# An edge loop of a graph layer: score pieces and codes moved earlier in the hand-written order, and one-hots turned by a product of code columns

## Chip, cores and metric

The kernel runs on one core of a Trainium2 chip. The metric is the device time of one execution in microseconds (us), the median of several runs. Engines are named as the profile names them: PE (TensorE, with PEld its weight loads), DVE (VectorE), ACT (ScalarE), POOL (GpSimd, which here issues the gathers), SP (SyncE, which issues other DMAs).

## The reference, cut to what matters

The whole program is a stack of four graph layers, each followed by a feed-forward layer with experts, over 1250 nodes of 512 features and 20000 edges sorted by target node. The change is in the second graph layer (L1), attention over the edges with four heads:

```
h = (x @ W).reshape(n, 4, 128)
alpha = leaky_relu(a_src[src] + a_dst[dst] + a_edge, 0.2)    # one score per edge and head
amax  = segment_max(alpha, dst)
ex    = exp(alpha - amax[dst])
denom = segment_sum(ex, dst)
out   = segment_sum(h[src] * (ex / (denom[dst] + 1e-16)), dst) + bias
```

After it come a normalisation over the nodes and the residual sum. Everything is float32 from outside.

## The kernel before, in words

The edges are laid out in groups of 512, each padded so that all its targets lie in one block of 125 nodes. 46 groups are run without a condition, as 23 pairs (group A is the even one of a pair, B the odd one); four more groups stand under a condition (L1836) that this input does not meet. A table t1 in device memory holds for each node the 4 x 129 features (with a column of ones) and four source scores.

For a group g the loop `l1_edges` (L1688 to L1918) does these steps, each a small function:

- `gathers` (L1709, the DMA is L428): POOL issues four indirect DMAs that bring the 512 source rows into G. The buffer ring has eight groups.
- `onehot` (L1720): DVE compares target numbers with 0..124 and makes `oh`, 128 edges x 4 x 125 nodes, float32.
- `pieces` (L1725): for a pair, DVE adds the gathered source score and the edge score, and splits the float32 sum into three bfloat16 pieces (two adds L1732, then L1735, L1737, L1738, L1739). They go into columns 15 to 26 of CD; columns 0 to 14 hold the seven bits of the target's number, their complements and a one, made once in `edge_bits`.
- `coded` (L1741): PE transposes CD, eight blocks a pair, into `pc`, and ACT copies it to R: 27 rows x 1024 edges, bfloat16 (L1746).
- `spread` (L1754): for each head, one product of SEL (27 x 125) with R. It yields, for each node and edge, the edge's score if the edge has that target and a huge negative number if not.
- `maxima` (L1759): DVE takes the maximum along the edges, four reductions (L1765), then five small steps that update the running maximum of the block; `mn` is a copy for the next step.
- `turned` (L1748): PE transposes `oh`, four transposes into the PSUM bank `tr` (L1750), and ACT copies them to `ohT` (L1752).
- `fetched` (L1781): products with `ohT` as weights bring each edge its target's score and maximum (L1784). Float32 products appear as two PE instructions each. The results lie in the bank of the fourth head's spread.
- `lowered`, `weights_of` (L1775, L1787): the factors by which old sums shrink, and the weights ex of the edges (DVE L1790 to L1793, ACT L1794).
- `scaled`, `scaled_v` (L1800, L1806): ACT (28 instructions of 128x129 a pair) and DVE (one block a pair) multiply G by ex.
- `summed` (L1810): products of `oh` with G, 16 PE instructions a group, into the two banks `ac` (L1814).
- `added` (L1818): DVE adds them to the running sums ACC (L1823).

Three pairs are in flight: in turn i the loop computes the weights of pair i, sums pair i-1, takes the maxima of pair i+1, makes the pieces and codes of pair i+2, and starts the gathers of pair i+3. The order in which DVE, ACT and PE do these steps is written out by hand (L1857 to L1918): each engine gets its instructions in the order of the calls and runs them in that order, waiting where an operand is missing. In a turn with i >= 0 the order is, for PE: spread A (pair i+1), sums A (i-1), spread B, turned A, sums B, turned B, codes (i+2), fetched A and B. For DVE: weights (i), maxima A (i+1), one scaled block, adds A (i-1), maxima B, pieces (i+2), adds B, one-hots (i+2). For ACT: the exponential, five scaled blocks, the copy for turned A, two scaled blocks, the copy for turned B, the copy of R, the two lowering steps. POOL's gathers are not in the hand-written order but need free buffers, so they follow the sums.

`edge_bits` (L1638) runs much earlier, among the first expert layer's work: it makes the bit columns of CD, and SEL by four small transposes (L1683).

Of the kernel before, what the change touches and what calls it, by code (L numbers as in the profile page):

```python
# [9 lines left out]
F32 = mybir.dt.float32  # L10
F16 = mybir.dt.float16
BF16 = mybir.dt.bfloat16
# [3 lines left out]
AF = mybir.ActivationFunctionType  # L16
OP = mybir.AluOpType
# [6 lines left out]
P = 125  # L24
NT = N // P
EJ = E // P
GS = 512
# [9 lines left out]
class Net:  # L37
# [1600 lines left out]
    def edge_bits(self):  # L1638

        nc, ES, f = self.nc, self.ES, self.g1  # L1640
        nh, nb = 4, 7
        C = 2.0 ** 100
        nr = f.nr = 2 * nb + 1


        CD = f.CD = f.p.tile([128, ST, nr + 3 * nh], BF16, name="g1cd")
        SEL = f.SEL = f.p.tile([nr + 3 * nh, nh, P], BF16, name="g1sel")
        with ExitStack() as c3:
            r = self.pool(c3, "g1b")
            T = r.tile([128, nh, nr + 3 * nh], F32, name="g1t")  # L1650
            xp = r.tile([128, 1], I32, name="g1xp0")
            d0 = r.tile([128, ST], F32, name="g1d0")

            for t in (T[0:1, 0, 0:1], xp[0:1, :], d0[0:1, 0:1]):
                nc.vector.tensor_copy(t, self.S1[0:1, 0, 0:1])
            nc.vector.tensor_scalar(d0, ES[:, :, 1], float(2 ** nb - 1), None, OP.min)
            x = r.tile([128, ST], I32, name="g1x0")
            nc.vector.tensor_copy(x, d0)
            nc.vector.tensor_copy(xp, self.iota_p)
            nc.vector.memset(T, 0.0)  # L1660
            nc.vector.memset(T[:, :, 2 * nb:nr], -float(nb) * C)
            for h in range(nh):
                for j in range(3):
                    o = nr + j * nh + h
                    nc.vector.memset(T[:, h, o:o + 1], 1.0)
            nc.vector.memset(CD[:, :, 2 * nb:nr], 1.0)
            bt = r.tile([128, nb], F32, name="g1bt")
            xs = [x, r.tile([128, ST], I32, name="g1x1")]
            for b in range(nb):
                y = xs[1 - b % 2]  # L1670
                nc.vector.tensor_scalar(y, x, 1, None, OP.logical_shift_right)
                nc.vector.scalar_tensor_tensor(CD[:, :, b], y, -2.0, x, OP.mult, OP.add)
                nc.vector.tensor_scalar(CD[:, :, nb + b], CD[:, :, b], -1.0, 1.0, OP.mult, OP.add)
                yp = r.tile([128, 1], I32, name=f"g1yp{b}")
                nc.vector.tensor_scalar(yp, xp, 1, None, OP.logical_shift_right)
                nc.vector.scalar_tensor_tensor(bt[:, b:b + 1], yp, -2.0, xp, OP.mult, OP.add)
                x, xp = y, yp
            nc.vector.tensor_scalar(T[:, :, 0:nb], bt[:, None, :].to_broadcast([128, nh, nb]), C, None, OP.mult)
            nc.vector.tensor_scalar(T[:, :, nb:2 * nb], bt[:, None, :].to_broadcast([128, nh, nb]), -C, C,
                                    OP.mult, OP.add)  # L1680
            for h in range(nh):
                ps = self.bank("g1sel_ps")
                nc.tensor.transpose(ps[:nr + 3 * nh, :P], T[:P, h, :], self.ident[:P, :P])  # L1683
                nc.vector.tensor_copy(SEL[:, h, :], ps[:nr + 3 * nh, :P])
            identb = f.identb = f.p.tile([128, 128], BF16, name="g1id")
            nc.vector.tensor_copy(identb, self.ident)

    def l1_edges(self, ctx):  # L1688
# [4 lines left out]
        nc, tc, ES, SI, f = self.nc, self.tc, self.ES, self.SI, self.g1  # L1693
        nh, ch, nr = 4, 128, f.nr
        tw = nh * (ch + 1) + nh
        ACC, AM, AE, t1, CD, SEL, identb = f.ACC, f.AM, f.AE, f.t1, f.CD, f.SEL, f.identb
        gq = self.pool(ctx, "g1g", bufs=8)
        q8 = self.pool(ctx, "g1h", bufs=8)
        q4 = self.pool(ctx, "g1p", bufs=4)
# [4 lines left out]
        tr = self.bank("oht_ps")  # L1704

        mg = mx[3][:, :16 * nh].rearrange("p (k h) -> p k h", k=8)
        st, pr = {}, {}

        def gathers(g, after=False):  # L1709
            G = gq.tile([128, 4, tw], F32, name="G")  # L1710
            ix, o = SI, 4 * g
            if after:

                ix, o = q8.tile([128, 4], I32, name="ix"), 0
                nc.vector.tensor_copy(ix, SI[:, 4 * g:4 * g + 4])
            for k in range(4):
                self.gather(G[:, k, :], t1, ix[:, o + k:o + k + 1])
            st[g] = {"G": G}

        def onehot(g):  # L1720
            oh = st[g]["oh"] = q8.tile([128, 4, P], F32, name="oh")
            nc.vector.tensor_tensor(oh, self.iota[:, None, :P].to_broadcast([128, 4, P]),
                                    ES[:, 4 * g:4 * g + 4, 1:2].to_broadcast([128, 4, P]), OP.is_equal)
# [22 lines left out]
            nc.scalar.copy(pr[i]["R"][:, j0 * GS:j1 * GS], pc[:nr + 3 * nh, j0 * GS:j1 * GS])  # L1746

        def turned(g):  # L1748
            for k in range(4):
                nc.tensor.transpose(tr[:P, k * 128:(k + 1) * 128], st[g]["oh"][:, k, :], self.ident)  # L1750
            ohT = st[g]["ohT"] = q4.tile([P, GS], F32, name="ohT")
            nc.scalar.copy(ohT, tr[:P, :])  # L1752

        def spread(g):  # L1754
            for h in range(nh):
# [72 lines left out]
        def at(f, i, *args):  # L1828
            if 0 <= i < NP:
                f(i, *args)  # L1830

        def one(f, i, j, *args):
            if 0 <= i < NP:
                f(2 * i + j, *args)
# [22 lines left out]
        with self.tc.manual_schedule(engines={E.DVE, E.Activation, E.PE}):  # L1857
            for j in range(2):
                gathers(j)
                onehot(j)  # L1860
                turned(j)
            for i in range(-2, NP + 1):


                at(weights_of, i)
                if i >= 0:
                    one(spread, i + 1, 0)
                kv = 2 if i == NP - 1 else 1
                one(scaled, i, 0, range(kv, 4))
                if i >= 0:  # L1870
                    one(maxima, i + 1, 0)
                if i in (-1, 0):
                    one(gathers, i + 3, 0, True)
                for k in range(kv):
                    one(scaled_v, i, 0, k)
                one(summed, i - 1, 0)
                if i > 0:
                    one(gathers, i + 3, 0)
                one(spread, i + 1, 1)
                one(added, i - 1, 0)  # L1880
                if i == NP - 1:
                    for k in range(2):
                        one(scaled_v, i, 1, k)
                else:
                    one(scaled, i, 1, range(0, 2))
                if i >= 0:
                    one(turned, i + 1, 0)
                one(scaled, i, 1, range(2, 4))
                one(summed, i - 1, 1)
                if i > 0:  # L1890
                    one(gathers, i + 3, 1)
                one(maxima, i + 1, 1)
                if i in (-1, 0):
                    one(gathers, i + 3, 1, True)
                if i == -1:
                    for j in range(2):
                        one(onehot, i + 2, j)
                if i == -2:
                    for j in range(2):
                        at(pieces, i + 2, j, j + 1)  # L1900
                        at(coded, i + 2, j, j + 1)
                        one(gathers, i + 3, j, True)
                        if j == 0:
                            one(spread, i + 2, 0)
                            one(maxima, i + 2, 0)
                else:
                    at(pieces, i + 2, 0, 2)
                if i >= 0:
                    one(turned, i + 1, 1)
                if i > -2:  # L1910
                    at(coded, i + 2)
                for j in range(2):
                    one(fetched, i + 1, j)
                at(lowered, i + 1)
                one(added, i - 1, 1)
                if i >= 0:
                    for j in range(2):
                        one(onehot, i + 2, j)  # L1918
# [468 lines left out]
```

## Time and profile before

| | us |
|---|---|
| median of 3 runs | 2721.48 |
| lowest and highest | 2719.5, 2733.79 |
| the profiled execution | 2716.28 |
| its span, first to last instruction | 2714.5 |
| PE busy in the span | 2444.6 (90%) |
| DVE busy | 1419.5 (52%) |
| mean granted TensorE clock | 0.923 |
| edge loop, 3rd to 22nd pair's start | 882.12 to 1172.61 |

How to read what follows: the timeline's lines give the start, the length, the engine, the line of the kernel, the operation, what it writes and reads, the shapes, and how many instructions were merged; in brackets stands the idle time before and what ended it. A line of the stretches gives from and to, the length, the busy time of each engine with the count of its instructions, the granted clock of PE as a share of full speed, the share of DMA engines in use and GB/s. A line of the waits gives who waited for whom, the total, how often, and the longest.

### The profile page before, as it was taken

The page shows a single profiled execution, that of the slowest core. Times are in us where ns is not written, and L with a number is a line of the kernel's source. Part 1 is how long each engine was busy: PE and PEld are TensorE (multiplying, and loading weights), DVE is VectorE, ACT ScalarE, POOL GpSimd, SP SyncE. Part 2 cuts the span into 40 slices and gives each one's busy share as a digit, 9 for nine tenths or more (in the row PEclk, how much of TensorE's full clock was granted, in tenths as well). Part 3 has the DMA queues.
Part 4 walks back from the last instruction along what each step waited for, and adds up shares of the span by engine and source line. Part 5 has one row for each costly group of instructions (what it writes and reads, how often), then busy time and mean ns, then how long its engine had stood idle before and what let it go on. Part 6 is the DMA issues. An engine that isn't in the chain of part 4 may idle for free.

```text
span 2714.5 us, 29769 instructions
## 1 busy us (share of the span) xinstructions
PE 2444.6 (90%) x10367; PEld 1550.5 (57%) x10367; DVE 1419.5 (52%) x3219; ACT 821.3 (30%) x1824; POOL 475.8 (18%) x540
## 2 busy tenths in 40 slices
PE   6899889999995999985879899999999799969996
PEld 3555689999944777764634454445554344445542
DVE  8766552100055888875257995567963663621000
ACT  4541111212124767752122342023421131211110
POOL 0002111211005445511120000100010121122211
PEclk9999669999996888895979899999999899979998
DMA  3112246666615445422832102310122201469997
GB/s 84 51 38 77 67 140 198 207 203 215 185 32 154 138 134 147 135 47 81 339 115 89 48 29 73 102 52 30 59 69 93 86 2 46 144 240 350 369 374 260
DMA packets 106745, 360.03 MB, mean 133 GB/s; under 512 B 34817, under 2 KB 39702, under 8 KB 84827
## 3 DMA queue, kind: packets, MB, share of 16 engines
q1 hardware_dynamic: 59867, 252.68, 26.5%
q0 software_dynamic: 44560, 100.92, 14.1%
q10 hardware_dynamic: 2160, 4.45, 0.5%
q8 instruction: 84, 1.38, 0.2%
q14 instruction: 74, 0.61, 0.1%
HBM read 328.36 MB, written 29.53 MB: 132 GB/s over the span
## 4 chain that ended last, share of the span: by engine, by line
PE 36%; DMA 9%; DVE 4%; issue 2%; ACT 1%; POOL 0%; POOLq 0%; SPq 0%; ACTq 0%; DVEq 0%
PE g_acc L1141 11%; PE g_ps L1097 7%; DMA f3wd<-in_L_ffn_W_down_dram 4%; PE f_ps L1616 3%; PE g_ps L1277 3%; PE f_ps L1590 2%; PE g_ps L1486 2%; DMA f3wd<-n_L_ffn_W_down_last_dram 1%; DMA f1ys<-f1y 1%; PE g_ps L1459 1%; PE g_ps L1464 1%; PE f_ps L1340 1%; DVE g_junk L1068 1%; PE g_ps L1040 1%; DMA CT<-in_L_ffn_W_down_dram 1%
## 5 line engine op out<-in xcount | busy, mean ns | idle before, releaser
L1141 PE MATMUL g_acc<-g_e,g2hh 125*128 125x417 f32 (+1 forms) x960 | 344.6, 519 | 7.4 <-DVE g_e L1131 7.4
L1141 PEld LDWEIGHTS g_acc<-g_e,g2hh 125*128 125x128 f32 x960 | 182.9, 192 | 166.7 <-issue 157.3
L1814 PE MATMUL ac_ps<-G,oh 128*125 128x258 f32 x736 | 199.4, 430 | 1.8 <-DVE g1acc L1823 1.5
L428 POOL DMA_INDIRECT G<-t,SI x160 | 156.0, 975 | 236.5 <-issue 100.0
L1804 ACT ACTIVATE G<-G,ex 128x129 f32<-128x129 f32 x632 | 190.1, 390 | 0.8
L1814 PEld LDWEIGHTS ac_ps<-G,oh 128*125 128x125 f32 x736 | 153.7, 215 | 46.0 <-issue 13.8
L564 PE MATMUL f_ps<-f0xgt,f0w 128*128 128x187 f32 x1024 | 168.8, 325 | 0.1
L575 PE MATMUL f_acc<-f0ht,f0w 128*128 128x187 f32 x1024 | 166.7, 325 | 0.0
L564 PEld LDWEIGHTS f_ps<-f0xgt,f0w 128*128 128x128 f32 x1024 | 165.5, 192 | 0.4 <-DVE f0xgt L105 0.3
L575 PEld LDWEIGHTS f_acc<-f0ht,f0w 128*128 128x128 f32 x1024 | 164.7, 191 | 0.3
L1125 DVE SCALAR_TENSOR_TENSOR g_e<-g_qb,g_a 125x1250 f32<-125x1250 f32 x80 | 120.4, 1515 | 69.3 <-DMA g_qb<-g_qd 61.7
L1126 ACT ACTIVATE g_e<-g_e,g_a 125x1250 f32<-125x1250 f32 x80 | 106.3, 1335 | 137.1 <-DVE g_e L1125 136.7
L1616 PE MATMUL f_ps<-f3wd,f3ht 128*39 128x512 f32 (+1 forms) x544 | 132.0, 609 | 14.8 <-DMA f3wd<-in_L_ffn_W_down_dram 14.7
L1622 DVE TENSOR_SCALAR f3y<-f_ps,f3k_wsel 39x512 f32<-39x512 f32 x32 | 24.0, 749 | 228.6 <-PE f_ps L1616 228.1
L1097 PE MATMUL g_ps<-g22w,g2ht 128*125 128x512 f32 x320 | 138.0, 593 | 0.2 <-DMA g22w<-in_L_gnn_W_dram 0.2
L224 PE MATMUL c_ps<-ohs,ohd 128*125 128x512 f16 (+1 forms) x552 | 108.7, 345 | 21.8 <-DVE ohd L215 13.3
L1068 DVE CUSTOM_DVE_ANT_0 g_junk<-g_mb,g_asb 125x1250 f32<-125x1250 bf16 x80 | 116.6, 1457 | 19.4 <-DMA g_asb<-g_as 15.2
L1131 DVE SCALAR_TENSOR_TENSOR g_e<-g_e,CT 125x1250 f32<-125x1250 f32 x80 | 115.8, 1450 | 7.1 <-ACT g_e L1126 6.8
L1765 DVE TENSOR_REDUCE gm<-mx_ps 125x1 f32<-125x512 f32 x184 | 113.9, 681 | 3.7 <-PE mx_ps L1756 3.7
L592 DVE TENSOR_SCALAR f0y<-f_ps,f0xg,f0r 128x512 f32<-128x512 f32 (+1 forms) x16 | 12.2, 802 | 187.2 <-PE f_ps L590 187.2
L218 DVE TENSOR_SCALAR ohs<-iota,ES 128x1250 f16<-128x1250 f16 x184 | 89.2, 541 | 34.9 <-PE c_ps L224 32.0
L224 PEld LDWEIGHTS <-ohd 128*125 128x125 f16 x552 | 69.5, 138 | 61.7 <-DVE ohd L215 14.1
(678 smaller groups left out, 3866.4 us busy)
## 6 DMA issues: line engine op xcount, KB each, us to landing
f0w<-in_L_ffn_w_dram SPq DMA_DIRECT2D x64, 1024.0 KB
f3wd<-in_L_ffn_W_down_dram SPq DMA_DIRECT2D x48, 1280.0 KB
CT<-in_L_ffn_W_down_dram SPq DMA_DIRECT2D x16, 1280.0 KB
f1w<-in_L_ffn_w_dram SPq DMA_DIRECT2D x13, 1024.0 KB
f3wu<-in_L_ffn_W_up_dram SPq DMA_DIRECT2D x12, 1024.0 KB
g_mb<-mbd POOLq DMA_DIRECT2D x40, 305.2 KB, 3.3
g_qb<-g_qd SPq DMA_DIRECT2D x16, 625.0 KB
f2tv<-in_L_ffn_tv_W_dram SPq DMA_DIRECT2D x16, 512.0 KB
```

What stands on the lines that cost most here:

```text
L224: nc.tensor.matmul(pss[i][:P, :cn], lhsT=ohd[g % 2][:, k, :], rhs=ohs[(4 * g + k) % R][:, c0:c0 + cn], start=g == 0 and k == 0, stop=k == ...
L428: self.nc.gpsimd.indirect_dma_start(out=out, out_offset=None, in_=table, in_offset=bass.IndirectOffsetOnAxis(ap=idx, axis=0))
L564: nc.tensor.matmul(ps[:, :cap], lhsT=w[:, k, f * 128:(f + 1) * 128], rhs=xgt[e][:, k, :], start=k == 0, stop=k == 3)
L575: nc.tensor.matmul(acc[e][d][:, :cap], lhsT=w[:, f, d * 128:(d + 1) * 128], rhs=ht[e][:, 4 * c + f, :], start=c == 0 and f == 0, stop=c == ...
L1068: nc.vector.tensor_tensor_reduce(junk, mb, asb[h], 1.0, -3e38, OP.add, OP.max, accum_out=mx[:, i, h:h + 1])
L1097: nc.tensor.matmul(ps[:P, :], lhsT=HT[:, k, i * P:(i + 1) * P], rhs=ws[hf][k // 4][:, k % 4, :], start=k == 0, stop=k == kt - 1)
L1125: nc.vector.scalar_tensor_tensor(e, qb[h][0], A8[:, s, h:h + 1], qb[h][1], OP.add, OP.max)
L1131: nc.vector.scalar_tensor_tensor(e, e, 1.0, self.CT[:, s, :], OP.min, OP.mult)
L1141: nc.tensor.matmul(accs[h][f][c][:, :cn], lhsT=H[:, s, h * 256 + f * 128:h * 256 + (f + 1) * 128], rhs=e[:, c0:c0 + cn], start=s == 0, sto ...
L1616: nc.tensor.matmul(ps[64 * h:64 * h + k, :], lhsT=ht[g][:n, f, j * k:(j + 1) * k], rhs=ws[h][:n, f - f0, :], start=f == 0, stop=f == nf - 1)
L1804: nc.scalar.activation(gv[:, k, h], gv[:, k, h], AF.Copy, scale=ex[:, k, h:h + 1])
L1814: nc.tensor.matmul(ac[j][:P, 0:2 * (ch + 1)], lhsT=v["oh"][:, k, :], rhs=v["G"][:, k, j * 2 * (ch + 1):(j + 1) * 2 * (ch + 1)], start=k == ...
```

## The change

It has three parts. First, `edge_bits` makes one more 27 x 125 matrix, SAME: its rows for bits and complements are the node's bits as 0 and 1, the row of ones is 1 - 7 = -6, and the rows of the pieces are 0. A product of SAME with R gives 1 where an edge's seven bits all agree with the node's, and 0 or less elsewhere. Second, `turned` is one such product, followed by a Relu on ACT, in place of four transposes and a copy; it now needs R. Third, the order: in turns with i >= 0 the pieces go ahead of maxima B, and the codes go ahead of the second half of scaled B and of sums B, right behind turned A. In the first two turns they stay where they were, and the first two `turned` come behind the first codes.

```diff
@@ edge_bits
+            SAME = f.SAME = f.p.tile([nr + 3 * nh, P], BF16, name="g1same")
+            O = r.tile([128, nr + 3 * nh], F32, name="g1o")
+            nc.vector.memset(O[:, nr:], 0.0)
+            nc.vector.tensor_scalar(O[:, :2 * nb], T[:, 0, :2 * nb], 1.0 / C, None, OP.mult)
+            nc.vector.memset(O[:, 2 * nb:nr], 1.0 - nb)
+            ps = self.bank("g1sel_ps")
+            nc.tensor.transpose(ps[:nr + 3 * nh, :P], O[:P, :], self.ident[:P, :P])
+            nc.vector.tensor_copy(SAME, ps[:nr + 3 * nh, :P])
@@ turned
-            for k in range(4):
-                nc.tensor.transpose(tr[:P, k * 128:(k + 1) * 128], st[g]["oh"][:, k, :], self.ident)
+            nc.tensor.matmul(tr[:P, :], lhsT=SAME, rhs=pr[g // 2]["R"][:, g % 2 * GS:(g % 2 + 1) * GS],
+                             start=True, stop=True)
             ohT = st[g]["ohT"] = q4.tile([P, GS], F32, name="ohT")
-            nc.scalar.copy(ohT, tr[:P, :])
+            nc.scalar.activation(ohT, tr[:P, :], AF.Relu)
@@ the order, ahead of the first turn
                 onehot(j)
-                turned(j)
@@ the order, in a turn
                 one(added, i - 1, 0)
+                if i == -2:
+                    for j in range(2):
+                        at(pieces, i + 2, j, j + 1)
+                        at(coded, i + 2, j, j + 1)
+                        one(gathers, i + 3, j, True)
+                        if j == 0:
+                            one(spread, i + 2, 0)
+                            one(maxima, i + 2, 0)
+                        one(turned, i + 2, j)
+                elif i >= 0:
+                    at(pieces, i + 2, 0, 2)
...
                 if i >= 0:
                     one(turned, i + 1, 0)
+                    at(coded, i + 2)
                 one(scaled, i, 1, range(2, 4))
                 one(summed, i - 1, 1)
...
                 if i == -1:
                     for j in range(2):
                         one(onehot, i + 2, j)
-                if i == -2:
-                    for j in range(2):
-                        at(pieces, i + 2, j, j + 1)
-                        at(coded, i + 2, j, j + 1)
-                        one(gathers, i + 3, j, True)
-                        if j == 0:
-                            one(spread, i + 2, 0)
-                            one(maxima, i + 2, 0)
-                else:
                     at(pieces, i + 2, 0, 2)
                 if i >= 0:
                     one(turned, i + 1, 1)
-                if i > -2:
+                if i == -1:
                     at(coded, i + 2)
```

More of the change, by code (lines that the diff above doesn't have):

```diff
@@ L1695, in l1_edges @@
         tw = nh * (ch + 1) + nh
-        ACC, AM, AE, t1, CD, SEL, identb = f.ACC, f.AM, f.AE, f.t1, f.CD, f.SEL, f.identb
+        ACC, AM, AE, t1, CD, SEL, SAME, identb = f.ACC, f.AM, f.AE, f.t1, f.CD, f.SEL, f.SAME, f.identb
         gq = self.pool(ctx, "g1g", bufs=8)
```

## The prediction

> **What bounds the kernel now.** The page's groups put the edge loop's sums (L1814, 199.4 us of PE) near the top, so I looked for the loop's stretch and cut it by stage. From the third pair's start (the DVE instruction L1790 at 882.12) to the 22nd (1172.61) there are 19 whole pairs. The three lines below are the busy time of each engine in that stretch and in two stretches of two pairs each. Columns: PE, PEld, DVE, ACT, POOL busy, then the granted clock.
>
> ```profile
> 882.12:1172.61 290.49, 276.17 (x1369) 211.44 (x1368) 243.74 (x743) 208.95 (x646) 141.96 (x146) 0.88 0.50 136
> 1003.92:1037.35 33.43, 32.13 (x145) 24.19 (x145) 25.99 (x79) 22.07 (x68) 15.48 (x17) 0.80 0.46 128
> 1131.09:1158.55 27.46, 25.78 (x145) 20.16 (x145) 25.31 (x79) 21.85 (x68) 15.72 (x17) 1.00 0.58 150
> ```
>
> The reader is to see two kinds of pair with the same work: 13.73 us (27.46/2) where the clock is 1.00, 16.72 (33.43/2) where it is 0.80. The mean is 290.49/19 = 15.29. At 1.00 DVE is the bound: 12.65 of 13.73 us busy, the rest gaps of some 30 ns between its instructions. At 0.80 DVE waits for PE. The waits of DVE in the 19 pairs:
>
> ```profile
> DVE g1acc L1823 <- PE ac_ps L1814: 24.0, 12, 2.7
> ```
>
> Where does the half clock come from? I cut PE's time into pieces of 3.41 us, at the places where the clock changes. First two pieces from a slow pair, then two from a fast one, then the share of the sums (L1814 alone) in two pieces:
>
> ```profile
> 1000.51:1003.92 3.41, 2.77 (x27) 2.46 (x27) 3.13 (x10) 1.90 (x4) 2.38 (x4) 1.00 0.74 214
> 1003.92:1007.34 3.42, 3.42 (x8) 1.96 (x8) 3.28 (x10) 2.44 (x9) 1.85 (x2) 0.50 0.69 181
> ...
> 1140.46:1143.87 3.41, 2.57 (x25) 2.21 (x23) 2.98 (x13) 2.20 (x6) 2.68 (x3) 1.00 0.74 193
> 1143.87:1147.28 3.41, 3.41 (x19) 2.51 (x19) 3.31 (x9) 1.89 (x9) 1.90 (x3) 1.00 0.71 218
> ```
> ```profile
> 908.35:911.76 3.41, 0.90 (x4) 0.81 (x5) 1.00 0.71 192
> 911.76:915.18 3.42, 3.42 (x10) 2.65 (x9) 0.50 0.39 112
> 1140.46:1143.87 3.41, 0.48 (x3) 0.07 (x1) 1.00 0.74 193
> ```
>
> A piece that holds the whole thin stretch of PE (turned, coded, fetched; no sums at all in 1000.51 to 1003.92) is followed by half clock; one that shares it with the sums is not. All the half-clock stretches here last one or two such pieces. The price: 2.99 us a pair for 2 x (1 - 0.80) x 16.72 = 6.7 us of half clock, 0.43-0.45 us each. In the mean pair 0.12 x 2 x 15.29 = 3.7 us are half.
>
> The piece at 908.35 says more. It has 0.90 us of sums and all four 27-row spreads (L1756, 375 ns each), and half clock follows; 1140.46 has 0.48 of sums, no spread, but four transposes and eight codes, and keeps full clock. So a 27-row product counts for little in whatever sets the clock.
>
> **The order, walked on a full-clock pair.** DVE and PE between 1144.82 (t = 0) and 1158.55 (t = 13.73):
>
> ```profile
> 1149.61 1.56 DVE L1823 SCALAR_TENSOR_TENSOR g1acc<-g1acc,co,ac_ps 125x129 f32 x4
> 1150.48 0.70 PE L1750 MATMUL oht_ps<-ident,oh 128*125 128x128 f32 x4
> 1151.02 3.65 PE L1814 MATMUL ac_ps<-G,oh 128*125 128x258 f32 x16
> 1151.09 2.48 DVE L1765 TENSOR_REDUCE gm<-mx_ps 125x1 f32<-125x512 f32 x4
> 1154.61 0.38 DVE L1732 TENSOR_TENSOR s<-G,g1ae 128x16 f32<-128x16 f32 x2
> 1155.69 0.20 DVE L1739 TENSOR_TENSOR g1cd<-rest,g1cd 128x32 bf16<-128x32 f32 x1
> 1155.85 1.57 DVE L1823 SCALAR_TENSOR_TENSOR g1acc<-g1acc,co,ac_ps 125x129 f32 x4
> 1155.95 0.62 PE L1743 MATMUL cd_ps<-g1id,g1cd 128*27 128x128 bf16 x8 [0.84 <-DVE g1cd L1739]
> 1156.50 1.95 PE L1784 MATMUL mx_ps<-mn,ohT 125*128 125x8 f32 x16
> ```
>
> DVE: weights 0, maxima A 0.75, adds A 4.79, maxima B 6.27, pieces 9.79 to 11.07, adds B 11.03, one-hots 12.52. PE: sums A 0.98 to 4.73, spread B, turned A, sums B 6.20 to 9.85, turned B, codes 11.13, fetched 11.68 to 13.63. Sums B touch no code and no piece: they run while DVE does maxima B.
>
> **The change, part by part.**
> *Turned.* Removed: per group four transposes, 0.60 to 0.70 us; added: one product of 27x125 by 27x512. No row has it, the nearest is L1756 of the same shape: 375 ns alone, 0.23 to 0.27 from start to start (1.07/4). PE gains 0.35 to 0.45 us a group, 0.8 a pair. At full clock DVE is the bound, so this is worth nothing by itself; where PE is late (12 of 19 pairs) it could give up to 0.8 x 12 = 10 us. I take 0, since the next item puts new waits around it. The Relu copy in place of L1752's copy (585 ns): the trace has Relu only on 8 columns (L1778, 203 ns), beside Exp and without a table load between. For 512 columns I bound it by 557 (the fastest L1752) and by 186 + 0.833 x 512 = 612 (the Trainium skill, "ScalarE: Activation LUTs", What ACT_TABLE_LOAD costs); either way ACT, 10.9 of 13.73 us busy, hides it.
>
> *Pieces ahead of maxima B.* On DVE the same six instructions, 1.28 us, go from t = 9.79 to 6.27: they end at 7.55 instead of 11.07. Maxima B and the mn that fetched needs come 1.24 later, 11.03. What they need is G, gathered a pair earlier. Its last gather would start 0.75 + 3 x 1.25 after the earlier pair's sums B and land 3.7 later, so 8.2 us after those sums; pieces come 8.6 after them. Cover 0.4 us; without it up to 0.5 us a pair (a gather took up to 6.2 us, but with eight queued back to back, which become two sets of four). I take 0.
>
> *Codes ahead of sums B.* This is the costly edit. PE runs its queue in order, so sums B now stand behind codes, which wait for the pieces, which wait for adds A, which wait for sums A. Codes start 0.06 after the last piece (1155.95 against 1155.89): 7.61. Sums B follow 0.55 later: 8.16 instead of 6.20, end 11.81. Adds B could start 0.41 before that end (1178.62, where sums A ended at 1179.03), 11.40; DVE is free at 11.03. DVE waits 0.37; behind it one-hots and the next weights. Full-clock pair: 14.10. Fetched, behind sums B and turned B, ends near 13.95, just covered. The copy of R on ACT goes ahead of scaled B's second half: ACT's slack of 2.8 us hides that.
>
> *The clock.* Before, PE had one thin stretch a pair: 9.85 to 14.71, with transposes and codes in it, and 1.5 us between sums A and B (4.73 to 6.20). After: two, 4.73 to 8.16 (spread B, turned A, 1.5 us idle, codes) and 11.81 to 15.08 (turned B, fetched, next spread), 3.4 and 3.3 us, each as long as a clock piece and poorer, since the transposes are gone. And now each half-clock stretch lands on a path with no slack: sums A, adds A, pieces, codes, sums B, adds B, one-hots, weights, sums A.
>
> I walked it: at full clock a half-pair is 7.05 us against two pieces of 6.83, so the pieces creep 0.22 forward until one lies in a thin stretch. Then 3.4 us are half, which adds 1.4; that moves the next thin stretch by 1.65 against the pieces, mostly into the next one, whose half clock lasts two pieces (+2.7), then one again, then two free half-pairs. That is 13.6 us half in 2.5 pairs, 5.4 a pair: 14.10 + 5.4 x 0.43 = 16.4, less about 0.4 that the DVE-bound start of a pair absorbs: 16.0. Over 19 pairs: 19 x (16.0 - 15.29) = +13.5 us.
>
> Here two rules of the Trainium skill speak otherwise ("TensorE: Matmul & The Clock Gate"). "Why this matters for your kernels" wants no PE gaps over some 3 us. No gap here exceeds 1.5, so by it nothing throttles and the pair is 14.10, -22.6 us; but before, the longest gap is 0.85 us in these slow pairs and half clock comes all the same. Part 4 says that transposes do not count as busy in the same way, so removing them could cost nothing; by the row 1140.46, with 0.48 us of sums, they and the codes do count. I go by the rows.
>
> *Prologue and setup.* Turned leaves the prologue's head, which has this:
>
> ```profile
> 818.39 1.28 ACT L1752 ACT_TABLE_LOAD   x1 [0.87 <-PE oht_ps L1750]
> ```
>
> That lay under the wait for the first gathers (to 830.49). The first ACT work is now the copy of R at 832.22, and if the load goes with it, +1.28 us; 0 if it is issued earlier. I take 1.2. The setup adds five small DVE instructions and a transpose amid the L0 experts: a cast of 0.27, memsets of 0.06 to 0.15, about 0.8 in all, where DVE was 1.6 of 10 us busy; PE 0.15. I take 0.3, ends 0 and 1.
>
> Sum: 13.5 + 1.2 + 0.3 = +15 us. The profiled execution took 2716.28 us (span 2714.5), so 2731; the median shown is 2721.48, 5.2 above: 2737.
>
> **Rivals.** *The clock holds*: if 27-row products count in full, thin stretches hold 0.85 us more of work and the clock seldom falls. Pairs of 14.1 to 14.6: -22.6 to -13, with +1.5: 2700 to 2710, faster. It decides from 2.8 us of half clock a pair downward ((15.29 - 14.10)/0.43). For it: pairs without half clock exist before. Against: 908.35. *Some half clock*, 14.6 to 15.6: 2710 to 2729, about no change. *Heavy*: two-piece stretches in most half-pairs, or gathers late as well, 16.7 to 18: +27 to +51, 2750 to 2775. *It does not free PE*: the turned product waits for tr or R; R is made a pair ahead, so I give that nothing of its own.
>
> **How the numbers follow.** Likeliest (15.6 to 16.6, 2729 to 2748) 0.42; heavy 0.16; some 0.26; clock holds 0.16. About 0.5% (13.6 us) is what a measurement can tell from no change. Faster: the clock-holding case and a part of the next, 0.20. Slower: heavy and two thirds of the likeliest, 0.45. Same: 0.35. The range leaves out half of the holding case and a part of the heavy one: 2702 to 2765.
>
> **What would show it.** Codes right after turned A, with PE idle some 1.5 us ahead of them, and DVE waiting for sums B at adds B: the serial path. Half clock in the 19 pairs at a third of the time (mean clock near 0.83): the clock step. If the mean clock is 0.95 or more I am wrong on the sign. If pairs at full clock take 13.7, the wait of sums B is hidden. If DVE waits for G at L1732, the gather cover failed.

## The result and the profile after

| | before | after |
|---|---|---|
| median of 5 runs, us (lowest to highest) | 2721.48 (2719.5 to 2733.79) | 2751.55 (2751.01 to 2752.12) |
| ratio of the times, 95% interval | | 1.0088 (1.0061 to 1.0114) |
| the profiled execution (its span) | 2716.28 (2714.5) | 2751.57 (2749.7) |
| start of the 3rd and of the 22nd pair | 882.12, 1172.61 | 883.08, 1201.27 |
| the mean pair (full clock; half clock in it) | 15.29 (13.73; 3.59) | 16.75 (14.11; 6.11) |

The changed kernel is slower by some 1%: the ratio is clear of 1, and the medians lie 30 us apart. The profiled executions lie 35.3 us apart. 28.7 of these are there when the 22nd pair starts: 27.7 in the 19 pairs, 1.0 at the third pair. The other 6.6 come late, most of it in the last expert layer, where the code is the same; runs of the kernel before differ by 14 us among themselves, so I read nothing into them.

These are stretches of the profile after, with the columns of the prediction's first fence: the 19 pairs, one pair at full clock, one of the many slow ones.

```profile
883.08:1201.27 318.19, 293.19 (x1255) 214.93 (x1254) 242.25 (x742) 209.86 (x646) 143.43 (x147) 0.82 0.46 125
897.21:911.31 14.10, 12.53 (x67) 9.29 (x68) 12.53 (x40) 10.94 (x34) 7.79 (x9) 1.00 0.55 153
1047.68:1064.71 17.03, 15.80 (x67) 11.60 (x68) 12.86 (x41) 11.05 (x34) 7.81 (x9) 0.80 0.45 126
```

See in the counts that PE and ACT did the same work in both pairs (67 and 34 instructions); only the clock differs. From 911.31 on 13 of the 17 pairs take 17.02 to 17.11 us from start to start, and nearly all hold 6.83 us of half clock. The clock changes at the bounds of pieces of 3.413 us (six of them below are 20.48), and five such pieces are 17.07 us: the loop has locked to the pieces of the clock, and the same two of five are half each time. Cut into pieces of 3.41 us, the slow pair shows why. The two columns of busy time are here those of the sums alone (PE, PEld, L1824), then the clock:

```profile
1046.26:1049.67 3.41, 1.00 (x5) 0.88 (x6) 1.00 0.37 93
1049.67:1053.09 3.42, 3.42 (x10) 2.64 (x9) 0.50 0.73 214
1053.09:1056.50 3.41, 1.02 (x5) 0.55 (x3) 1.00 0.02 9
1056.50:1059.91 3.41, 2.40 (x6) 1.91 (x7) 0.50 0.69 176
1059.91:1063.32 3.41, 2.52 (x12) 1.83 (x10) 1.00 0.44 135
1063.32:1066.74 3.42, 1.04 (x5) 0.92 (x6) 1.00 0.43 101
```

Each piece with about 1.0 us of sums is followed by a half one, each with 2.4 or more by a full one; the sixth piece is the first again. The first holds fetched and spread A beside its sums, the third spread B, turned A and the idle time ahead of the codes: the two thin stretches of the prediction. Here is that pair in the timeline:

```profile
1048.67 5.44 PE L1824 MATMUL ac_ps<-G,oh 128*125 128x258 f32 x16
1053.71 1.57 DVE L1833 SCALAR_TENSOR_TENSOR g1acc<-g1acc,co,ac_ps 125x129 f32 x4 [1.14 <-PE ac_ps L1824]
1054.04 1.07 PE L1766 MATMUL mx_ps<-R,g1sel 27*125 27x512 bf16 x4
1054.95 0.37 PE L1759 MATMUL oht_ps<-R,g1same 27*125 27x512 bf16 x1
1055.36 0.60 ACT L1762 ACTIVATE ohT<-oht_ps 125x512 f32<-125x512 f32 x1 [0.51 <-PE oht_ps L1759]
1056.55 1.03 PE L1752 MATMUL cd_ps<-g1id,g1cd 128*27 128x128 bf16 x8 [1.23 <-DVE g1cd L1748]
1057.52 4.92 PE L1824 MATMUL ac_ps<-G,oh 128*125 128x258 f32 x16
1062.04 1.57 DVE L1833 SCALAR_TENSOR_TENSOR g1acc<-g1acc,co,ac_ps 125x129 f32 x4 [1.98 <-PE ac_ps L1824]
1062.36 0.42 PE L1759 MATMUL oht_ps<-R,g1same 27*125 27x512 bf16 x1
```

Sums A and B take 5.44 and 4.92 us where they took 3.75 and 3.65: one half-clock piece lies in each. DVE waits for both (1.14 and 1.98). Codes wait 1.23 us for the pieces, and sums B follow right behind them. That is the serial path that the prediction walked. Over the 19 pairs DVE's waiting at the adds more than doubled, from 24.0 us in 12 waits to:

```profile
DVE g1acc L1833 <- PE ac_ps L1824: 55.4, 36, 2.7
```

### The profile page after: what moved, and what is told of

Read it like the earlier page. It is cut to its first block, busy times and chain, and to the rows that moved or that the text cites. A ratio compares the mean times of both kernels' runs of the same rounds, so it can differ in the third digit from the quotient of the medians.

```text
span 2749.7 us, 29500 instructions
## 1 busy us (share of the span) xinstructions
PE 2464.9 (90%) x10230; PEld 1550.0 (56%) x10230; DVE 1419.1 (52%) x3223; ACT 822.6 (30%) x1824; POOL 476.1 (17%) x540
## 4 chain that ended last, share of the span: by engine, by line
PE 49%; DMA 9%; DVE 8%; issue 2%; ACT 1%; POOL 0%; DVEq 0%; POOLq 0%; ACTq 0%; SPq 0%
PE g_acc L1141 11%; PE ac_ps L1824 7%; PE g_ps L1097 7%; DMA f3wd<-in_L_ffn_W_down_dram 4%; PE f_ps L1616 3%; PE g_ps L1277 2%; PE g_ps L1486 2%; PE f_ps L1590 2%; DMA f3wd<-n_L_ffn_W_down_last_dram 2%; PE mx_ps L1794 1%; PE g_ps L1459 1%; DMA f1ys<-f1y 1%; PE g_ps L1464 1%; PE f_ps L1340 1%; DVE g1acc L1833 1%
## 5 line engine op out<-in xcount | busy, mean ns | idle before, releaser
L1824 PE MATMUL ac_ps<-G,oh 128*125 128x258 f32 x736 | 224.9, 471 | 1.8 <-DVE g1acc L1833 1.5
L1824 PEld LDWEIGHTS ac_ps<-G,oh 128*125 128x125 f32 x736 | 169.7, 237 | 54.6 <-issue 14.2
```

Of the source, the lines that this page charges most:

```text
L1824: nc.tensor.matmul(ac[j][:P, 0:2 * (ch + 1)], lhsT=v["oh"][:, k, :], rhs=v["G"][:, k, j * 2 * (ch + 1):(j + 1) * 2 * (ch + 1)], start=k == ...
```

## The result on other chips

The experiments ran on other chips, and there the same program of the kernel before takes another time. (The chips of the experiments are known apart; which chip gave the result above is not known.)

| chip | before, median (range, runs) | after |
|---|---|---|
| the first, of the result above | 2721.48 (2719.5 to 2733.79, 5) | 2751.55 |
| second | 2827.54 (2824.84 to 2830.53, 7) | not run |
| third (a quarter of an hour later: 2828.83 in 14 runs) | 2829.61 (2817.96 to 2834.66, 39) | 2754.7 |
| fourth (whether it is the first is not known) | 2724.85 (2715.09 to 2741.12, 23) | not run |

So on the third chip the change is a gain: ratio 0.9755 (0.9728 to 0.9783). The changed kernel behaves alike on both (17.07 us pairs, 6.83 of them half). It is the kernel before that differs; hence its own profile on the third chip. Its 19 pairs take 96 us more there, of 113 in the whole span. No chip was seen both with these slow pairs and without them, so a cause that goes with the time of the run and not with the chip is not excluded. Two waits of the stretch of the loop, then one pair's timeline, with the waits in brackets ("remote" stands where the view finds no releaser on this core):

```profile
ACT R L1746 <- remote: 103.5, 18, 6.0
DVE ex L1790 <- remote: 57.7, 17, 3.5
```
```profile
1030.73 0.62 PE L1743 MATMUL cd_ps<-g1id,g1cd 128*27 128x128 bf16 x8 [0.64 <-issue]
1031.28 2.16 PE L1784 MATMUL mx_ps<-mn,ohT 125*128 125x8 f32 x16
1036.64 1.00 ACT L1746 COPY R<-cd_ps 27x1024 bf16<-27x1024 bf16 x1 [5.84 <-remote]
1036.80 0.19 DVE L1790 TENSOR_TENSOR ex<-s,mx_ps 128x32 f32<-128x32 f32 x1 [3.42 <-remote]
1037.69 1.86 PE L1756 MATMUL mx_ps<-R,g1sel 27*125 27x512 bf16 x4 [4.25 <-ACT R L1746]
```

PE's records end codes at 1031.35 and fetched at 1033.44. Yet the copy of R, which waits for the codes, starts at 1036.64, and the next weights, which wait for fetched, at 1036.80. I call this the hold: the end of the codes becomes known 5.3 us after their record, that of fetched 3.4 us after. The trace also keeps the times at which semaphores were raised (counters that one engine raises and another waits for). PE's own, on which both wait, is raised at 1036.61 and at 1036.77, each 0.03 us before the waiter starts. So neither ACT nor DVE was slow to answer: PE's signal came late, or, since the ends of PE's instructions are modelled in the profile, its work did. Meanwhile PE stands idle for over 4 us (4.25 here), and half clock comes with it. In the first chip's profile of the same kernel, in the fast pair of the prediction, the codes end at 1156.57, the semaphore is raised at 1156.58, and the copy of R follows:

```profile
1156.61 1.00 ACT L1746 COPY R<-cd_ps 27x1024 bf16<-27x1024 bf16 x1 [0.88 <-PE cd_ps L1743]
```

To compare the profiles, take from the mean pair 0.43 us per us of half clock (the prediction's price) and call the rest the base. Where pairs without half clock exist in number, the base lies at or a little above them. In the runs with the hold it is a sum and no more: no pair there is without half clock, and on the third chip each pair of the kernel before holds 10.24 us at full clock, so that a us more of half clock goes with a us more of pair. The 19 pairs after the second, in each profile:

| kernel | chip | pair | half clock | base |
|---|---|---|---|---|
| before | first | 15.29 | 3.59 | 13.74 |
| after | first | 16.75 | 6.11 | 14.12 |
| before | third | 20.36 | 10.12 | 16.01 |
| after | third | 16.84 | 6.29 | 14.14 |
| order only | second | 14.87 | 1.26 | 14.33 |
| 128 rows | second | 15.04 | 1.44 | 14.42 |
| codes back | second | 19.24 | 9.00 | 15.37 |
| turned only | second | 19.34 | 9.10 | 15.43 |
| before, 128 rows | third | 20.09 | 9.67 | 15.93 |
| spread out | third | 14.31 | 0.18 | 14.23 |
| before, no gathers | third | 14.95 | 3.78 | 13.33 |
| before, fetched split | third | 20.47 | 10.23 | 16.07 |
| before, filler | third | 16.67 | 5.73 | 14.20 |
| order and 128 rows | fourth | 14.91 | 1.08 | 14.45 |

The base sets the profiles with the hold (15.4 to 16.1) apart from all others (13.3 to 14.5), among which the changed order with its serial path has 14.1 to 14.5. The half-clock column shows what each kernel makes of the clock.

## Experiments: which part of the change costs

**One part taken back or alone.** Codes back behind turned B; the new turned step in the old order; the new order with the old transposes.

```diff
 codes back (of the changed kernel):
                     one(turned, i + 1, 0)
-                    at(coded, i + 2)
...
                 if i >= 0:
                     one(turned, i + 1, 1)
-                if i == -1:
+                if i >= -1:
                     at(coded, i + 2)
 order only (of the changed kernel), in turned:
-            nc.tensor.matmul(tr[:P, :], lhsT=SAME, rhs=pr[g // 2]["R"][:, g % 2 * GS:(g % 2 + 1) * GS],
-                             start=True, stop=True)
+            for k in range(4):
+                nc.tensor.transpose(tr[:P, k * 128:(k + 1) * 128], st[g]["oh"][:, k, :], self.ident)
```

> The changed kernel with one edit undone: the codes go back behind turned B; the pieces stay early and the one-hots are still turned by a product. Clock theory (two thin stretches of PE a pair each catch one 3.4 us piece of half clock, since 27-row products count for little; the serial path only passes it on): sums B are free of the codes, a pair at full clock is 13.7 instead of 14.1, but the one thin stretch that is left holds turned B, codes, fetched and the next spread with no transposes, so it is caught in every pair: 6.8 us half, a pair of 16.4 to 16.8, the whole 2738 to 2750. Queue theory (sums B behind the codes are the cost by themselves): the loss is gone, 2695 to 2722.

> The kernel before with one part of the change alone: one-hots turned by the product with SAME; pieces and codes where they were before. Clock theory: PE has 0.8 us less to do a pair, but the thin stretch loses the transposes that counted, so nearly every pair gets 6.8 us of half clock instead of 3.7 in the mean: pairs of 16.0 to 16.7, the whole 2733 to 2750. Queue theory: the part is free or a small gain where PE was late, 2708 to 2722.

> The changed kernel with the transposes in place of the product: the new order alone. Clock theory: the serial path stays, 14.1 to 14.5 a pair at full clock; each of the two thin stretches is richer by 0.43 us of transposes, so the pieces are caught less often: pairs of 15.3 to 16.5, 2722 to 2745. Queue theory: as the whole change, 2745 to 2755. If the product alone is the cause: 2715 to 2725.

Measured on the second chip: codes back 2801.84, turned only 2805.5, order only 2717.5 us, against 2827.54 before there. Ratios 0.9907 (0.9889 to 0.9925), 0.9923 (0.9907 to 0.994), 0.9614 (0.9598 to 0.9631). The first two missed what either theory gave: both keep the codes right ahead of fetched, as before, and both show the hold (the copy of R starts up to 4.2 and 3.1 us after the codes). So what the product alone costs in the old order, on a chip without the hold, was not measured. Order only is the telling one. Its 19 pairs, to be read against the first line of the profile after:

```profile
887.19:1169.71 282.52, 257.58 (x1369) 199.93 (x1367) 239.93 (x742) 208.41 (x646) 143.74 (x147) 0.96 0.52 141
```

Its path is as serial as that of the changed kernel, and its pairs are 14.1 to 14.6 where no half clock falls, as in 12 of 19. It takes 2717.5 where the changed kernel took 2751.55 and 2754.7 on two other chips: under the 2722 to 2745 of the clock theory, and in the band of the third guess, that the product is the cause. So the new order by itself is not what makes the changed kernel slow. With the transposes back, half clock falls from 6.11 us a pair to 1.26: in this order they keep the clock up, and the product in their place does not.

**The rows of the products.** In the changed kernel SEL, SAME and R get 128 rows: zeros below row 27 of SEL and SAME, ones in R. The results are the same and so is the number of PE instructions.

```diff
-        SEL = f.SEL = f.p.tile([nr + 3 * nh, nh, P], BF16, name="g1sel")
+        SEL = f.SEL = f.p.tile([128, nh, P], BF16, name="g1sel")
+        nc.vector.memset(SEL, 0.0)
...
+        Rs = [qr.tile([128, 2 * GS], BF16, name=f"R{j}") for j in range(2)]
+        for t in Rs:
+            nc.gpsimd.memset(t, 1.0)
```

> The changed kernel with the 27-row products (spread and turned) made 128 rows deep: SEL and SAME are padded with rows of zeros, R with rows of ones, so the results stay and each product takes as long as before. If products of few rows count for little in what sets the clock, the two thin stretches now hold 1.1 us and 1.3 us more that counts: half clock nearly gone, pairs of 14.1 to 14.8, 2700 to 2715. If rows don't matter to the clock: 2749 to 2754, unchanged.

Measured: 2715.34 us, ratio 0.9607 (0.9591 to 0.9623). The stretch of its 19 pairs:

```profile
883.36:1169.14 285.78, 239.19 (x1254) 190.59 (x1253) 239.35 (x742) 207.87 (x646) 143.17 (x147) 0.95 0.51 139
```

PE, DVE and ACT do as many instructions as in the changed kernel to within one (1254, 742, 646), but the clock is 0.95 in place of 0.82. The order and the products are those of the changed kernel; only the rows differ. So what these products are worth to the clock hangs on their rows. One reserve stands for this run and for order only: the changed kernel itself was not run on the second chip. It took nearly the same on the first and the third (2751.55 and 2754.7), which makes another time there unlikely.

**Both cures at once.** Order only, with the spread at 128 rows as well.

> The changed kernel with both cures: transposes in place of the product (as in the order-only run) and the spread padded to 128 rows. Theory that the half clock comes from thin stretches whose 27-row products count for little: half clock under 1 us a pair, pairs 14.1 to 14.5, 2700 to 2712 us, some 40 to 50 us below the changed kernel on any chip. If something else of that order sets a remainder of half clock, the pair stays at the 14.9 to 15.0 of either cure alone, 2714 to 2720 us.

Measured on the fourth chip: 2722.44 us, ratio 0.9984 (0.9967 to 1.0002), no difference from the kernel before on that chip. Half clock is 1.08 us a pair, but pairs stay at 14.91: the cures don't add up, and both totals forecast were too low. Six pairs still hold one half piece and take 16.0 to 17.0, more than the 14.1 + 1.5 of the price. In the three longest, the pieces' first step waits for a late gather; in the changed kernel, with its longer pairs, it never does:

```profile
DVE s L1747 <- DMA G<-t,SI: 2.3, 3, 1.1
```

What sets the rest of the remainder was not tested. The run shows that one cure takes most of what is to be had. It also shows no gain of the new order where, by the time of the kernel before, there is no hold: the base is 0.4 to 0.7 us above the 13.74 of before in all forms of the order, and here that takes back 0.7 of the 1.1 us a pair that the half clock gives.

## Experiments: what the hold is

**The two kernels again, and the kernel before with 128 rows**, on the third chip.

> The kernel before itself, for a profile on the chip of the other runs of this set, since its time there was 2827 and not 2721. If the difference lies in the clock of the edge loop: its pairs take near 20 us with 10 us half (as with the codes put back and with the product alone), and the other stages differ by less than 10 us in all. If the chip is slower throughout: every stage is longer by the same share, 4%.

> The changed kernel itself on the same chip. Clock theory: the pair at full clock is 14.1 on any chip, and what changes between chips is how much half clock the thin stretches catch; with two pieces a pair it stays near 17.1 and 2750, with more it goes to 20 and 2810. Queue theory: it keeps its distance of 30 us above the kernel before on every chip.

> The kernel before with one edit of the clock's diet alone: spread made 128 rows deep (SEL padded with zeros, R with ones), transposes and order as before. Clock theory: the thin stretch holds 0.85 us more that counts, half clock nearly gone, pairs of 13.7 to 14.3, 2688 to 2708. If rows don't matter: as the kernel before on the same chip.

Measured: the kernel before against itself 2830.3 (ratio 1.0006), changed 2754.7, before with 128 rows 2820.83, ratio 0.9973 (0.9963 to 0.9982). The last missed by far: the hold is there all the same (copy of R some 5.2 us after the codes in 16 of 19 pairs, PE idle for up to 4.4), and half clock stays at 9.67 us a pair.

**Before without its gathers.** From the ninth group on the rows of the first eight groups are used again, so the loop computes other sums than the reference.

```diff
+            if 8 <= g < NM:
+                st[g] = {"G": kept[g % 8]}
+                return
```

> The kernel before without the gathers of groups 8 to 45 (left out; those groups reuse the rows of groups 0 to 7), so its edge loop moves almost nothing. On a chip where the kernel before takes some 2829 us. Theory that the gathers hold PE's end signals: the copy of R no longer waits long past the codes, pairs fall from 20.5 to 13.7-16 us, 2690 to 2745 us. Theory that the hold comes from PE's own order of work (16 small products right behind the codes): waits of the R copy of 3 to 6 us stay, pairs 18 to 20.5, 2790 to 2830 us.

**Before, with fetched A ahead of the codes**, and **before, with four dense PE instructions a pair** between sums B and turned B, whose result is thrown away.

```diff
+                one(fetched, i + 1, 0)
                 if i > -2:
                     at(coded, i + 2)
-                for j in range(2):
-                    one(fetched, i + 1, j)
+                one(fetched, i + 1, 1)
```
```diff
                 one(summed, i - 1, 1)
+                if 1 <= i < NP:
+                    u = st[2 * i - 1]
+                    for k in range(2):
+                        nc.tensor.matmul(tr[:P, 0:2 * (ch + 1)], lhsT=u["oh"][:, k, :],
+                                         rhs=u["G"][:, k, 0:2 * (ch + 1)], start=True, stop=True)
```

> The kernel before with one step moved on PE: the first group's eight fetched products go ahead of the codes, so that only the second group's follow them. Theory that the hold needs all 16 small products behind the codes: no wait of the R copy over 2 us, pairs 14 to 16.5, 2700 to 2750 us. Theory that it is the starved stretch of PE as a whole (half clock, no dense work near): the wait stays, pairs 18 to 20.5, 2790 to 2830 us.

> The kernel before with four more dense PE instructions a pair (two float32 products of 128x258, some 0.9 us) between sums B and turned B; they repeat part of the sums and are thrown away. Clock theory: the thin stretch holds 0.9 us more dense work, fewer pieces are half, and the pair gets shorter although work is added: 14.6 to 16.5, 2710 to 2760 us. If dense work is not what is missing, each pair gets up to 0.9 us longer: 2829 to 2850 us.

Measured on the third chip, against 2828.83 of the kernel before beside them: 2717.79, 2829.42 and 2753.68 us. Ratios 0.9604 (0.9583 to 0.9624), 1.001 (0.9998 to 1.0023), 0.9725 (0.9698 to 0.9752). The waits of the copy of R in the three, in that order:

```profile
ACT R L1753 <- PE cd_ps L1750: 6.6, 19, 0.7
```
```profile
ACT R L1746 <- remote: 100.2, 17, 7.2
```
```profile
ACT R L1746 <- remote: 4.8, 1, 4.8
```

Without gathers the hold is gone from all pairs. Having fetched in two halves does nothing, so the idea that it takes all 16 small products behind the codes falls. The filler takes the hold from all but one pair, although it is work added: 75 us won by doing more. I had written that down as a test of the clock, and as such it decides nothing, since the hold went at the same time. It also weakens the run without gathers: a small shift in time ends the hold with the gathers in place, and leaving them out shifts the times too, so it is not shown that the gathers themselves hold PE's signal. In most pairs of the filler the codes end some 1.0 us before the next gather starts on POOL, in most of the held pairs of before some 0.3; but that distance does not decide it: the kernel before on the first chip often has the same 0.3 and no hold, and codes back has 1.2 in most pairs, with the hold.

So far shown: PE's signal comes late; it falls on the orders that leave codes and fetched together behind sums B, is absent where sums B follow the codes (changed, order only, 128 rows), where PE's work around the codes was spread or filled and in the one run without gathers, and it was met on the second and third chip and not on the first. What holds the signal back, and what differs between those chips or times, stays open.

**A version that beats both.** From the 128-row kernel: sums by output bank, sums B in two halves, turned B and fetched A between them, the codes behind them. Fetched goes to spare columns of the second sums bank, so that the next spread need not wait.

```diff
-        mg = mx[3][:, :16 * nh].rearrange("p (k h) -> p k h", k=8)
+        mg = ac[1][:, 512 - 16 * nh:].rearrange("p (k h) -> p k h", k=8)
...
-                one(summed, i - 1, 1)
+                one(summed, i - 1, 1, range(0, 1))
+                if i >= 0:
+                    one(turned, i + 1, 1)
+                    one(fetched, i + 1, 0)
+                one(summed, i - 1, 1, range(1, 2))
+                if i >= 0:
+                    at(coded, i + 2)
```

> A version meant to beat both: the changed kernel with 128-row products, codes behind sums B, and PE's thin work spread out: the results of fetched get room in a bank of the sums, so that turned B and fetched A can run between the two halves of sums B, and the next spread no longer waits for the weights. DVE keeps the early pieces. Clock theory: no thin stretch is longer than 2.6 us, no half clock after the start, pairs of 13.7 with DVE full, 2686 to 2698. If something else bounds the pair, it stays above 14.1: over 2700.

Measured on the third chip: 2702.71 us (2693.66 to 2705.45), ratio 0.9555 (0.9527 to 0.9583), and 52 us under the changed kernel there. Its 19 pairs:

```profile
882.07:1153.90 271.83, 234.95 (x1255) 179.80 (x1254) 242.00 (x742) 205.74 (x646) 143.48 (x146) 0.99 0.54 145
```

One pair of 19 holds a half piece, as the clock theory had it. But pairs without one take 14.2, not the 13.7 expected, so something else bounds them: the waits show sums held for adds, 33.1 us in 19 waits, 1.7 a pair, which I did not take apart. It was run on one chip only, and a part of its gain over the kernel before there is the hold that it avoids.

## The prediction, step by step

- *The serial path, 14.10 at full clock*: right. Pairs at full clock took 14.13 and 14.11; codes wait for the pieces and sums B for the codes, as walked. DVE waits for PE at adds B.
- *The clock, 5.4 us of half clock a pair*: right in mechanism, too small. The walk let the pieces of the clock creep through the pair, with two free half-pairs in five. In fact the loop locked: 14.1 + 6.83 x 0.43 = 17.04, which is five pieces within 0.03 us, so the pattern repeats itself. 6.83 in place of 5.4 is the mis-sized term, in the pairs that lock; with the first pairs, which were free, the mean is 6.11 and the 19 pairs cost +27.7 us in place of +13.5. The mean clock came out at 0.82, near the forecast 0.83, only because the pair grew along with its half clock.
- *0.4 us absorbed at the start of a pair*: not seen; the free pairs' 14.12 plus the price of 6.11 us gives the whole of the mean pair (14.12 + 2.63 = 16.75).
- *27-row products count for little*: borne out by the run with 128 rows. The rival "the clock holds" was thus wrong for the kernel as it is. That variant comes near it: 11 of its 19 pairs are free of half clock, but at 15.04 us a pair and 2715 us it lies in the band of "some half clock".
- *The two rules weighed against the trace*: both would have misled. The longest PE gap in the slow pair is 1.23 us ahead of the codes, and in the 19 pairs 1.6, far under the Trainium skill's 3 us ("TensorE: Matmul & The Clock Gate", Why this matters for your kernels); yet two pieces of five are half. And the transposes, which by Part 4 of that page do not count as busy in the same way, keep the clock at 0.96 over the 19 pairs of order only where the 27-row product lets it fall to 0.82.
- *Turned, worth 0 by itself*: the product took 0.37 and 0.42 us, the Relu copy 0.60 (the prediction's estimate was 557 to 612 ns). As a step of PE it was costed rightly; its real price, in this order, is what it takes from the clock.
- *Cover of the gathers, 0*: right for the kernel as it is, where DVE never waits for G at the pieces; but its pairs are 17 us long. In the run with both cures, at 14.91, it waits in three pairs.
- *Prologue and setup, 1.2 + 0.3*: 1.0 at the third pair's start. The table load came where it was feared, behind the wait for the codes:

```profile
832.12 1.28 ACT L1755 ACT_TABLE_LOAD   x1 [13.17 <-PE cd_ps L1752]
```

- *The total*: 2737 forecast, 2751.55 measured, inside the range of 2702 to 2765, though 3.6 us above the likeliest band. By its mean pair, 16.75, it stands at the low edge of what was called heavy (16.7 to 18, chance 0.16), but not for heavy's causes: half clock came almost always in single pieces, and no gather was late. The total has 14.2 us of the mis-sized clock and the late 6.6 against it, and the 5.2 us added from profile to median, which the runs after don't show (median and profiled execution are alike), for it.
- Not foreseen at all: that the kernel before is 4% slower on some chips. The forecast was made from a profile without the hold, and the measurement came from a chip without it; that was luck, since on the third chip the sign is the other one.

## What to carry to other kernels

Where the engine's clock follows its work, ask of each step what it is worth to the clock, not only how long it takes: a short product with few rows can cost more than the longer transposes that it replaces, and padding its rows to 128 cost nothing that showed here. Spread thin PE work between dense work rather than put it together, and see whether the loop's period comes to a whole number of clock pieces, where a bad pattern locks in. A consumer that starts long after its producer's record ends is a sign of its own; before a verdict on a change, time the kernel before on a second chip.

## What the runs showed of the hardware that was not expected

- Period locking: most pairs at 17.0 to 17.1 us (five pieces of 3.413) in the changed kernel on two chips; ten of 19 at 20.46 to 20.57 (six pieces, three of them half) in the kernel before on the third.
- The hold: PE's semaphore is raised 5.2 to 5.3 us after the record of the codes ends, in 17 of 19 pairs of the kernel before on the third chip; up to 4.2 us after it in two variants on the second; 0.01 us after it on the first, and in the run without gathers.
- The same program took 2721.48, 2827.54, 2829.61 and 2724.85 us in the sets of runs on the chips above.
- The 27-row products, padded to 128 rows, took no longer (spread 382 ns and turned 378 in the mean, against 386 and 400), and the mean clock of the loop was 0.95 in place of 0.82.
